# A layer of selected experts on one core: sums, splits and conditions at other places

## The chip, the cores and the metric

The kernel runs on one NeuronCore of a Trainium2 chip. The metric is the device time of one execution in microseconds. A core has TensorE (PE, with its weight loads shown apart as PEld), VectorE (DVE), ScalarE (ACT), GpSimd (POOL) and SyncE (SP). Each takes its instructions in its own order and waits on semaphores; SP only issues DMAs here.

## What is computed

`x` is 128 rows of 64 tokens of 256 numbers (float32). There are five routed experts, one chosen per row by `itok`, and two shared experts that every token passes. Each is a dense layer of 256 to 1024, a relu, and one of 1024 to 256.

```python
def _L0_cond_ref(x, type_label, wi, wo, swi, swo, g1, g2):
    s0 = _dense(x, swi[0], swo[0])          # relu(x @ wi) @ wo
    s1 = _dense(x, swi[1], swo[1])
    h = jax.nn.relu(jnp.einsum('bsd,bdf->bsf', x, wi[type_label]))
    eo = jnp.einsum('bsf,bfd->bsd', h, wo[type_label])
    gate_in = jnp.concatenate([eo[:, 0], s0[:, 0], s1[:, 0]], axis=-1)
    w = jax.nn.softmax(jax.nn.relu(gate_in @ g1) @ g2, axis=-1)[:, :, None, None]
    return eo * w[:, 0] + s0 * w[:, 1] + s1 * w[:, 2]

x = x + _L0_cond_ref(x, itok, ...)
# then one step of diffusion: y is x seen as 128 grids of 64 x 256, reflected at the borders
x = x + zX * lap_x(y) + zY * lap_y(y) + zR * y * (1.0 - y)
```

## The kernel before, in words

**Numbers in two parts.** A product in float32 precision is made of three PE matmuls: every operand is split in a high part (fp32r) and a low part, and high x high, high x low and low x high are added up. A split is one ACT copy (high part) and one subtraction on DVE or POOL (low part). What the relu gives is split likewise: in `hidden`, ACT's relu writes the high part and a DVE `scalar_tensor_tensor` the low part.

**Items and units.** Work on 512 tokens by one expert is an item. Its first layer isn't done as 8 products of blocks but by a scheme with 7 products (`A11` to `S4` of weights, `B11` to `T4` of tokens), which needs sums of weight blocks (`wsum`, `sum_wi`) and of token blocks (`xt`, `sum_x`) in advance. An item has four units (`unit`, q = 0 to 3). Each makes 7 products of 3 matmuls 128x512 into three PSUM tiles pa, pb and pd:

- pa = A11 B11; ACT copies it into pb
- pb += S2 T2; ACT copies pb to u2 in SBUF (records call it u); pa += A12 B21 gives the unit's first hidden tile
- pb += S3 T3 (after the u2 copy, since it writes the same tile), pd = S1 T1; ACT copies pb to u3; DVE adds c22 = pd + u3
- pb += A22 T4 gives a hidden tile, c22 is another; pd += S4 B22 (after c22, which reads pd), and pd + u2 is the fourth

The relu and low part of the fourth are put in the list `late` and issued after the first ACT copy of the next unit. Between the products stand the second layer's matmuls of the unit before (`gaps`, matmuls acc<-wo,h). They are 512 columns wide for the high part of h, 256 for the low part, which comes last. At an item's end the rows of the second half of tokens (`h_0b` to `h_7b`) follow, row after row into new PSUM tiles. Six PSUM tiles rotate for pa, pd and the accumulators, two for pb.

**Hooks.** Everything else is issued at fixed places in the program: `at(k, work)` puts work at hook k mod 4 of unit k // 4 of the item. `run(hooks[j])` stands in `unit`; hooks 16 and 17 are after the fourth unit. The order on every engine is then the program's order (`Ordered.on`, `keep`).

**Sequence.** Items 0 and 1 are the two shared experts on the first 512 tokens (to about 86 us), then five items of routed experts, numbered from EI = 100 (about 86 to 294 us, 41.57 us each), then a stream of nine smaller groups of rows (`stream(0, NRUN)`, about 294 to 443 us). In it each group takes 8 steps f: `up` (first layer, plain), `down` (second layer) two steps later, and `ahead` for loads and splits of the next group. Groups have 8 rows or 4; group 3 (HALF) is half as wide as the narrow ones (2 rows, 128 columns). In the stream ACT's, DVE's and POOL's instructions aren't held in program order (`in_order(False)`): a scheduler places them, PE's and the DMAs keep theirs. Groups 9 to 11 are needed only when the rows fall badly among the experts; a condition on a value read from the table (`total[0]`) guards them, and they don't run with these inputs. Then the shared experts' other token tiles are items 2 to 15 (41.34 us each), in which the outputs of the routed experts are gathered by POOL, summed with the gates, diffused (`diffuse_a`: ACT and POOL; `diffuse_b`: three DVE steps per half) and stored.

**Names in the records.** `wi` and `wsr`: split and raw weights; `x` and `xr`: split and raw tokens; `xt`: token sums; `gw`, `gwr`, `gh`, `gacc`: weights, raw weights, hidden and accumulators of the groups; `lq`, `la`, `lb`: the diffusion's tiles; h_0 to h_7 with a or b: hidden tiles of an item, a for the first half of the tokens. A matmul recorded as acc<-wo,h_0b reads such a tile. Nearly all records carry line 93 (`mm`) or line 108 (`keep`), so that tiles tell them apart; the condition is line 1124.

Of the kernel before, what the change touches and what calls it, by code (L numbers as in the profile page):

```python
# [21 lines left out]
NB = 4  # L22
# [27 lines left out]
def cond_resid_kernel(ctx: ExitStack, tc: tile.TileContext, xg, xs, xn, itok, z, we, ws, g1, g2, out):  # L50
# [580 lines left out]
    def product(dst, w, i, x, start, stop):  # L631
        for j, (wp, xp) in enumerate(((0, 0), (0, 1), (1, 0))):
            mm(dst, w[:, wp, i, :], x[:, xp, :], start and j == 0, stop and j == 2)

    def hidden(store, key, src):
        h = slot4(f"h{key[0]}_{key[1]}{'ab'[store is hb]}")
        act.activation(h[:, 0, :], src, AF.Relu)
        vec.scalar_tensor_tensor(h[:, 1, :], src, 0.0, h[:, 0, :].bitcast(F32), ALU.max, ALU.subtract)
        store[key] = h
# [9 lines left out]
    def unit(n, q, gaps, hooks):  # L649
        p = tokens(n)  # L650
        w = wip.pop(n * NQ + q)
        f = 2 * q
        pa = psum(f"pa{n}_{q}")
        pb = seeded(f"pb{n}_{q}")
        product(pa, w, A11, xop[p, B11], True, False)
        act.activation(pb, pa, AF.Copy)
        finish_late()
        run(gaps[0])
        run(hooks[0])
        product(pb, w, S2, xop[p, T2], False, False)  # L660
        product(pa, w, A12, xop[p, B21], False, True)
        u2 = slot2(f"u2_{n}_{q}")
        act.activation(u2, pb, AF.Copy)
        hidden(ha, (n, f), pa)
        run(gaps[1])
        run(hooks[1])
        product(pb, w, S3, xop[p, T3], False, False)
        pd = psum(f"pd{n}_{q}")
        product(pd, w, S1, xop[p, T1], True, False)
        u3 = slot2(f"u3_{n}_{q}")  # L670
        act.activation(u3, pb, AF.Copy)
        c22 = slot2(f"c22_{n}_{q}")
        vec.tensor_tensor(c22, pd, u3, ALU.add)
        run(gaps[2])
        run(hooks[2])
        product(pb, w, A22, xop[p, T4], False, True)
        product(pd, w, S4, xop[p, B22], False, True)
        hidden(hb, (n, f + 1), c22)
        hidden(ha, (n, f + 1), pb)
        vec.tensor_tensor(pd, pd, u2, ALU.add)  # L680
        late.append(lambda: hidden(hb, (n, f), pd))
        run(hooks[3])

# [270 lines left out]
    def ahead(g, f):  # L954

        if g >= NRUN:
            return
        if f == 0:
            if g == NRUN - 3:
                slots = nc.values_load(  # L960
                    tab[0:1, NSLOT + NU : NSLOT + NU + 1], min_val=0, max_val=NSLOT,
                    skip_runtime_bounds_check_because="the table's entries are bounded on the chip",
                )
                total.append(slots)
            if g + 1 < NRUN:
                if g <= NBIG and g != HALF:
                    load_group_w(g + 1)
                if g != HALF:
                    load_group_x(g + 1)
            if g < 2:  # L970
                reload(g)
            for u in range(3 * g, min(3 * g + 3, 2 * NQ)):
                load_wo(u)
            if g == NRUN - 2:
                load_x(1)
            if g == NRUN - 1:
                load_wi(2, 0)
                load_wi(2, 1)
                load_row()
        if f == 5 and g < 2:  # L980
            again(g)
        if g + 1 == HALF and f == 4:
            load_group_x(g + 2)
        if f == 6 and (g + 1 == HALF or NBIG <= g < NRUN - 2):
            load_group_w(g + 2)
        if g == 0 and f + FIRST < NF:
            split_group_w(0, f + FIRST)
        if g == HALF + 1 and f + 6 < NF:
            split_group_w(g, f + 6)
        if g + 1 < NRUN:  # L990
            if f == (0 if g == HALF else 4):
                split_group_x(g + 1)
            if g != HALF or f < 6:
                split_group_w(g + 1, f)
        elif f < 7:
            if f < 4:
                sum_x(1, T1 + f, gps)
            split_x(1, (B11, B21, T2, T3, T1, T4, B22)[f], vec)
# [19 lines left out]
    def at(k, *work):  # L1018

        return {divmod(k, 4): list(work)}  # L1020
# [64 lines left out]
    def next_fours(n, sums, splits):  # L1085
# [12 lines left out]
        at(3, lambda: load_fours(EI)),  # L1098
        at(8, lambda: dma(zt, z)),
        at(11, clear_spare, lambda: dma(g1t, g1), lambda: dma(g2t, g2)),  # L1100
        next_fours(EI, (10, 12, 14, 15), (15, 16, 16, 16, 16, 17, 17)),
    )
    left = item(1, left, bg)

# [16 lines left out]
    in_order(False)  # L1121
    stream(0, NRUN)

    with tc.If(total[0] > UH * NB):  # L1124
        for g in range(NRUN, NG):
            load_group(g)
            split_group_x(g)
            for f in range(NF):
                split_group_w(g, f)
            stream(g, g + 1)  # L1130
# [13 lines left out]
    def next_x(p):  # L1144
        if p == NP:
            return {}
        if p == 2:
            sums, splits, eng, slow = (8, 9, 10, 11), (12, 15, 14, 16, 16, 17, 16), gps, (B11, B21, B22)
        else:
            sums, splits, eng, slow = (10, 12, 14, 15), (15, 16, 16, 16, 16, 17, 17), vec, (B22,)  # L1150
        return join(
            at(4, lambda: load_x(p)),
            *(at(k, lambda i=i: sum_x(p, i, eng)) for i, k in zip((T1, T2, T3, T4), sums)),
            *(
                at(k, lambda i=i: split_x(p, i, gps if i in slow else vec))
                for i, k in zip((B11, T2, B21, T3, T1, T4, B22), splits)
            ),
        )

    def diffusion(t, k, with_halo=True, second=3, steps=(0, 1, 2)):  # L1160
        parts = [at(k, lambda: halo(t))] if with_halo else []
# [23 lines left out]
    for p in range(1, NP):  # L1185
        ta, tb = 2 * p, 2 * p + 1
        for e in range(2):
            n = 2 * p + e
            parts = [ahead_w(n)]
            if n == 2:  # L1190
                load_gate()
                parts.append(at(0, gate_shared))
                parts.append(at(1, gate_hidden_s))
                parts.append(at(4, lambda: load_y(0)))
                parts.append(at(5, step_factors))
                parts.append(at(4, gate_expert))
                parts.append(at(6, gate_hidden_e, lambda: load_y(2)))
                parts.append(at(7, lambda: load_sh(0)))
                parts.append(at(8, lambda: load_eo(0)))
                parts.append(at(9, lambda: load_y(3)))  # L1200
                parts.append(at(10, gate_weights))
                parts.append(sums(0, 11))
                parts.append(at(12, lambda: load_eo(2)))
                parts.append(at(13, lambda: load_y(1)))
                parts.append(at(16, lambda: load_sh(1)))
                parts.append(starts(ta, 17, 0))
            elif n == 3:
                parts.append(at(0, lambda: load_eo(3), lambda: load_eo(1)))
                parts.append(sums(1, 1))
                parts.append(starts(tb, 5))  # L1210
                parts.append(diffusion(0, 7, True, 4))
                parts.append(at(12, lambda: halo(1)))
                parts.append(next_x(2))
            elif n == 4:
                parts.append(at(2, lambda: load_y(4)))
                parts.append(diffusion(1, 0, False))
                parts.append(at(6, lambda: load_eo(4)))
                parts.append(diffusion(2, 6))
                parts.append(at(9, lambda: load_y(5)))
                parts.append(at(11, lambda: load_eo(5)))  # L1220
                parts.append(starts(ta, 14))
                parts.append(starts(tb, 16, 0))
            elif e == 0:
                parts.append(at(0, lambda t=ta: load_y(t), lambda t=ta: load_eo(t)))
                parts.append(at(4, lambda t=tb: load_y(t), lambda t=tb: load_eo(t)))
                parts.append(diffusion(ta - 2, 2))
                parts.append(starts(ta, 10))
                parts.append(starts(tb, 13))
            else:
                parts.append(diffusion(ta - 1, 2))  # L1230
                parts.append(next_x(p + 1))
            if n == 2 * NP - 1:
                parts.append(at(4, lambda: load_last(n)))
                parts.append(at(8, lambda: split_last_w(n)))
                parts.append(at(9, lambda: split_last_x(n)))
                parts.append(at(10, diagonals))
                parts.append(at(12, lambda: halo(ta)))
            left = item(n, left, join(*parts))
# [38 lines left out]
```

## Time and profile before

| | us |
|---|---|
| median of 3 executions | 1040.71 (1039.96 to 1044.65) |
| the profiled execution | 1041.6 |
| its span, from the first to the last record | 1039.9 |
| granted PE clock | 1.00 |
| idle time of DVE ahead of c (c22), mostly until ACT's u | 43.7 |
| idle time of ACT ahead of u, mostly until PE's pb | 111.0 |

The profile is of one execution. A row of the timeline is "start, duration, engine, line, operation, output<-inputs, shape, count", with the idle time before it and what ended it in brackets; one row may stand for several instructions. A row of the waits is "engine, tile, line <- engine, tile, line: us in all, times, longest". A matmul's record lasts longer than the distance to the next one, since matmuls are pipelined; the distance between two starts is what it costs.

Three stretches matter for the change. The table of busy times by stretch has them in this order: the half-width group, the condition, the second shared item (length, then busy time and instructions of each engine):

```profile
core 0: us, PE busy (x) PEld busy (x) DVE busy (x) ACT busy (x) POOL busy (x), PEclk, DMA share, GB/s
363.30:376.10 12.80, 11.89 (x88) 10.92 (x87) 10.97 (x26) 8.88 (x24) 0.00 (x0) 1.00 0.78 255
441.30:445.20 3.90, 1.88 (x12) 1.42 (x10) 0.76 (x2) 0.38 (x1) 0.00 (x0) 1.00 0.04 8
70.50:84.00 13.50, 12.67 (x63) 10.16 (x62) 12.91 (x28) 8.44 (x20) 0.00 (x0) 1.00 0.99 348
```

### The profile page before, as it was taken

To read this page: it belongs to the slowest core of one execution; us is meant where nothing else is said; L and a number is where in the kernel's file an instruction comes from. 1 tells how busy PE (TensorE), PEld (TensorE's weight loads), DVE (VectorE), ACT (ScalarE), POOL (GpSimd) and SP (SyncE) were. 2 spreads that over 40 slices of the span, in tenths; PEclk is the share of its full clock that TensorE was granted. 3 is DMA by queue.
4 is the path that set the end of the run, shared out by engine and by line. 5 is a ranking of instruction groups with operands and counts; after the bars stand their busy time and mean duration, and the time that the engine had idled before them with its cause. 6 is when DMAs were issued, how large, how long until landed. Compare 5 with 4: busy or idle time off the path is not lost.

```text
span 1039.9 us, 15667 instructions
## 1 busy us (share of the span) xinstructions
PE 1030.5 (99%) x5423; PEld 882.1 (85%) x5423; DVE 810.6 (78%) x1502; ACT 571.5 (55%) x1080; POOL 154.3 (15%) x165
## 2 busy tenths in 40 slices
PE   9999999999999999999999999999999999999998
PEld 7878888888888889978888888888888888888888
DVE  7997977988768575747889778678688688688776
ACT  6476666776656565643654545446355364355362
POOL 3000000000013100211432220212212102022020
PEclk9999999999999999999999999999999999999999
DMA  6477233331458765556435435334344163253321
GB/s 217 173 269 249 77 104 94 105 122 52 132 170 307 271 207 172 181 182 219 158 127 177 137 110 200 122 122 167 112 168 154 65 227 122 81 191 138 117 77 46
DMA packets 67123, 159.15 MB, mean 153 GB/s; under 512 B 7680, under 2 KB 34688, under 8 KB 67040
## 3 DMA queue, kind: packets, MB, share of 16 engines
q1 hardware_dynamic: 64512, 149.46, 41.8%
q0 software_dynamic: 2384, 8.52, 2.5%
q8 instruction: 44, 0.72, 0.3%
q14 instruction: 39, 0.32, 0.1%
q10 hardware_dynamic: 144, 0.13, 0.0%
HBM read 126.75 MB, written 31.33 MB: 152 GB/s over the span
## 4 chain that ended last, share of the span: by engine, by line
PE 57%; DVE 0%; ACT 0%; issue 0%; DVEq 0%
PE acc L93 30%; PE pb L93 11%; PE pd L93 7%; PE pa L93 7%; PE pu L93 1%; PE lin_b L93 0%; PE pgs L93 0%; PE gacc L93 0%; PE lin_c L93 0%; PE pge L93 0%; DVE lq L108 0%; DVE c L108 0%; ACT pb L108 0%; DVE end_qb L108 0%; PE pl L93 0%
## 5 line engine op out<-in xcount | busy, mean ns | idle before, releaser
L93 PE MATMUL pb<-x,wi 128*128 128x512 f32 x729 | 208.0, 393 | 0.6 <-ACT u L108 0.3
L108 ACT ACTIVATE u<-pb 128x512 f32<-128x512 f32 x162 | 96.9, 598 | 111.0 <-PE pb L93 107.9
L93 PEld LDWEIGHTS pb<-x,wi 128*128 128x128 f32 x729 | 130.4, 189 | 26.0 <-ACT u L108 3.5
L93 PE MATMUL pd<-x,wi 128*128 128x512 f32 x486 | 137.9, 392 | 0.1
L93 PE MATMUL pa<-x,wi 128*128 128x512 f32 x486 | 136.9, 390 | 0.0
L108 DVE SCALAR_TENSOR_TENSOR yb<-acc,wgt,yb 128x256 f32<-128x256 f32 x216 | 99.3, 482 | 18.1 <-PE acc L93 14.3
L108 ACT ACTIVATE pb<-pa 128x512 f32<-128x512 f32 x81 | 47.2, 582 | 115.5 <-PE pa L93 114.6
L93 PEld LDWEIGHTS pd<-x,wi 128*128 128x128 f32 x486 | 90.9, 188 | 21.9 <-DVE c L108 1.9
L93 PEld LDWEIGHTS pa<-x,wi 128*128 128x128 f32 x486 | 89.9, 188 | 17.8
L108 DVE TENSOR_TENSOR c<-pd,u 128x512 f32<-128x512 f32 x81 | 55.9, 690 | 43.7 <-ACT u L108 32.6
L93 PE MATMUL up<-gxh,gw 128*128 128x512 f32 (+2 forms) x288 | 73.4, 329 | 0.0
L108 POOL TENSOR_TENSOR la<-yb 128x508 f32<-128x508 f32 (+1 forms) x28 | 32.2, 1150 | 260.5 <-ACT yb L108 259.0
L93 PE MATMUL gacc<-gw,gh 128*128 128x512 f32 (+1 forms) x272 | 60.7, 363 | 2.9 <-PEq L1124 2.0
L93 PEld LDWEIGHTS gacc<-gw,gh 128*128 128x128 f32 x272 | 47.4, 188 | 11.6 <-issue 2.3
L93 PE MATMUL acc<-wo,h_0b 128*128 128x256 f32 (+1 forms) x172 | 56.5, 332 | 0.6 <-DVE h_6b L108 0.6
L108 DVE TENSOR_TENSOR gw<-gwr,gw 128x512 fp32r<-128x512 f32 x72 | 53.1, 780 | 5.0 <-ACT gw L108 4.9
L93 PE MATMUL acc<-wo,h_6b 128*128 128x256 f32 (+1 forms) x172 | 56.7, 334 | 0.0
L93 PE MATMUL acc<-wo,h_1b 128*128 128x256 f32 (+1 forms) x172 | 56.7, 333 | 0.0
L93 PE MATMUL acc<-wo,h_7b 128*128 128x256 f32 (+1 forms) x172 | 56.7, 333 | 0.0
L93 PE MATMUL acc<-wo,h_2b 128*128 128x256 f32 (+1 forms) x172 | 56.6, 333 | 0.0
L93 PE MATMUL acc<-wo,h_5b 128*128 128x256 f32 (+1 forms) x172 | 56.5, 332 | 0.0
L93 PE MATMUL acc<-wo,h_4b 128*128 128x256 f32 (+1 forms) x172 | 56.5, 332 | 0.0
(254 smaller groups left out, 2458.3 us busy)
## 6 DMA issues: line engine op xcount, KB each, us to landing
wi<-wi_d SPq DMA_DIRECT2D x55, 896.0 KB, 4.6
gwr<-we_in SPq DMA_DIRECT2D x32, 512.0 KB, 5.0
wsr<-we_in SPq DMA_DIRECT2D x20, 512.0 KB, 5.2
xr<-xs_in SPq DMA_DIRECT2D x32, 256.0 KB, 5.2
yb<-xn_in SPq DMA_DIRECT2D x16, 512.0 KB, 5.8
y_out<-lq SPq DMA_DIRECT2D x30, 256.0 KB, 2.2
wi_d<-wi SPq DMA_DIRECT2D x8, 896.0 KB, 4.5
xr<-xg_in SPq DMA_DIRECT2D x80, 64.0 KB, 2.0
```

The costliest lines, as they stand in the source:

```text
L93: nc.tensor.matmul(out_ap, lhsT=lhsT, rhs=rhs, start=start, stop=stop, skip_group_check=True)
L108: ins = call(*args, **kwargs)
```

## The change

1. In `unit`, pd += u2 stands ahead of the two `hidden` calls whose low parts DVE makes, so that on DVE the sum comes first. The `hidden` of pd itself stays in `late`.
2. In `ahead`, while group 3 (the half-width one) runs, weights of group 4 are split for f = 0 to 3 and no longer for 0 to 5; during group 4 the parts f + 4 are split and not only f + 6.
3. In item 1, three of the four token sums for the first routed item go one hook earlier (12, 14, 15 become 11, 12, 14), and the split of B11 goes from hook 15 to 16.
4. Each of the three seldom-run groups has a condition of its own, with the same test.
5. In item 4 the diffusion of tiles 1 and 2 is placed by the new function `diffusion_at`: the first half of tile 1 keeps its hooks, its second half's steps go from 5, 6, 7 to 6, 6, 7; the steps of tile 2 go from 8, 9, 10 and 11, 12, 13 to 8, 10, 10 and 11, 12, 14. `halo(2)` is issued behind the load at hook 6, not with the diffusion.

PE's order of matmuls stays as it was. On SP two stores of a routed item's output are issued two token loads later, and branches are added on every engine.

```diff
@@ unit
         product(pd, w, S4, xop[p, B22], False, True)
+        vec.tensor_tensor(pd, pd, u2, ALU.add)
         hidden(hb, (n, f + 1), c22)
         hidden(ha, (n, f + 1), pb)
-        vec.tensor_tensor(pd, pd, u2, ALU.add)
         late.append(lambda: hidden(hb, (n, f), pd))
@@ ahead
-        if g == HALF + 1 and f + 6 < NF:
-            split_group_w(g, f + 6)
+        if g == HALF + 1 and f + 4 < NF:
+            split_group_w(g, f + 4)
         if g + 1 < NRUN:
             if f == (0 if g == HALF else 4):
                 split_group_x(g + 1)
-            if g != HALF or f < 6:
+            if g != HALF or f < 4:
                 split_group_w(g + 1, f)
@@ item 1
-        next_fours(EI, (10, 12, 14, 15), (15, 16, 16, 16, 16, 17, 17)),
+        next_fours(EI, (10, 11, 12, 14), (16, 16, 16, 16, 16, 17, 17)),
@@
-    with tc.If(total[0] > UH * NB):
-        for g in range(NRUN, NG):
+    for g in range(NRUN, NG):
+        with tc.If(total[0] > UH * NB):
             load_group(g)
             split_group_x(g)
             for f in range(NF):
@@
+    def diffusion_at(t, starts, steps):
+
+        parts = []
+        for half in range(2):
+            parts.append(at(starts[half], lambda half=half: diffuse_a(t, half)))
+            for step in range(3):
+                parts.append(at(steps[half][step], lambda half=half, step=step: diffuse_b(t, half, step)))
+        return join(*parts)
@@ item 4
-                parts.append(diffusion(1, 0, False))
+                parts.append(diffusion_at(1, (0, 3), ((2, 3, 4), (6, 6, 7))))
                 parts.append(at(6, lambda: load_eo(4)))
-                parts.append(diffusion(2, 6))
+                parts.append(at(6, lambda: halo(2)))
+                parts.append(diffusion_at(2, (6, 9), ((8, 10, 10), (11, 12, 14))))
```

## The prediction

> **What bounds the kernel now.** I read the page's busy line and chain first. The chain names the engine that sets the end.
>
> ```profile
> PE 1030.5 (99%) x5423; PEld 882.1 (85%) x5423; DVE 810.6 (78%) x1502; ACT 571.5 (55%) x1080; POOL 154.3 (15%) x165
> ...
> PE 57%; DVE 0%; ACT 0%; issue 0%; DVEq 0%
> ```
>
> TensorE is busy 99% of a span of 1039.9 us and nothing else stands in the chain. No matmul is added or removed, so only PE's gaps can change. A busy share hides them, because a record lasts longer than the step to its successor: in the timeline of PE, steady matmuls start every 0.227 us with 512 columns (0.39 recorded) and every 0.120 us with 256. I took each start-to-start distance above these: 12.95 us in all. From the sixth token item on (after 560 us) there are only about 0.07 us per item of 41 us, so the change has nothing to win there, apart from 0.8 us at the tail, which it doesn't touch. Next came the lists of waits, of PE and of its weight loads, where a matmul's wait is often booked:
>
> ```profile
> PE gacc L93 <- PEq L1124: 2.0, 1, 2.0
> ...
> PE gacc L93 <- DVE gh L108: 0.9, 1, 0.9
> PE acc L93 <- DVE h_6b L108: 0.6, 1, 0.6
> ```
>
> ```profile
> PEld pb L93 <- ACT u L108: 3.5, 9, 0.7
> ...
> PEld pd L93 <- DVE c L108: 1.9, 5, 0.5
> ```
>
> Each is a place: the condition; the half-width group; the second shared item; the S3 product waiting for ACT's copy u (u2), which frees its PSUM tile; S4 waiting for c22. After each gap the second matmul comes another 0.11 late. The touched gaps, in us lost: 59.05 us (0.39), 74.72 (0.53), 102.08 (0.225), 144.0, 185.6, 227.1 (0.15 each), 268.7 (0.16), 517.1 (0.12), all S3; 83.87 (0.85, h_6b); 375.79 (1.16, gh); 445.13 (2.27, condition); 553.95 (0.38, c22). Together 6.5 us: the most that can be won.
>
> [...] 44 instruction packets of 16,384 B, one about every 24 us, and one at 442.22 us inside PE's branch, whose record runs from 441.225 for 3.73 us. [...] ACT's and DVE's records say 50 and 72 ns, but 0.45 and 0.59 us pass until their next instruction; I use those.
>
> **The change, part by part** (plus is slower).
>
> 1. *u2 ahead of the low parts.* Removed: two DVE operations between S4 and the sum. ACT's relu of pd, and the next unit's u2 copy queued behind it, come up to 1.2 us earlier.
>
> ```profile
> ACT h_6b L108 <- DVE pd L108: 23.6, 20, 1.7
> ```
>
> So the S3 gaps go: 0.84 in the routed items (102 to 269 us), 0.12 at 517, 0.92 in the shared items (counted in part 2). Added: the sum needs PE's last S4 matmul, the low parts did not. DVE waits in order, so everything behind waits too. Last unit of the second routed item:
>
> ```profile
> 161.72 0.69 DVE L108 TENSOR_TENSOR xt<-xr 128x512 f32<-128x512 f32 x1
> 162.33 0.69 DVE L108 SCALAR_TENSOR_TENSOR h_7b<-c,h_7b 128x512 fp32r<-128x512 f32 x1
> 162.93 0.69 DVE L108 SCALAR_TENSOR_TENSOR h_7a<-pb,h_7a 128x512 fp32r<-128x512 f32 x1
> 163.53 0.69 DVE L108 TENSOR_TENSOR pd<-pd,u 128x512 f32<-128x512 f32 x1
> ...
> 166.27 0.68 DVE L108 SCALAR_TENSOR_TENSOR h_6b<-pd,h_6b 128x512 fp32r<-128x512 f32 x1
> ```
>
> ```profile
> 161.91 0.85 PE L93 MATMUL pd<-x,wi 128*128 128x512 f32 x3
> ...
> 167.19 0.40 PE L93 MATMUL acc<-wo,h_0b 128*128 128x512 f32 x1
> ```
>
> DVE is free at 162.33; S4 starts at 161.91, and where c22 waits for such a product of three matmuls, DVE begins 0.97 after its start (PE at 451.87, DVE at 452.84 in the timeline): the sum starts at 162.88, and DVE runs 0.55 late. It has no idle until h_6b, which moves from 166.95 to 167.50. PE's matmul at 167.19 opens a new accumulator in the PSUM tile that pd leaves, so it waits for this very h_6b. New gap: 167.50 + 0.06 for the signal (h_6b ends at 83.81 and its matmul starts at 83.87) − 167.19 = 0.37, plus 0.11: 0.48, in the first four routed items (the fifth and the token items have no weight and token sums in between, and keep over 0.5 us of slack). 4 × 0.48 = +1.9. Routed items: −0.84 + 1.9 = **+1.07**. In other units c22 is 0.69 us ahead of S4 against a shift of 0.36 to 0.55, covered, and every unit starts anew from its own S4. Ends: −0.84 (margin half a microsecond larger than I read) and +2.5.
>
> 2. *Second shared item.* Three token sums and one split move a hook (a quarter of a unit), so DVE's work is spread differently; its stretch from 70.5 to 84 us is busy for 12.91 of 13.50. The first sum still waits for its DMA until 70.54. From there the new order is continuous: sum T1, pd's sum 71.15, two low parts, weight sums, T2, h_4b, wi, T3, h_6a, wi, c22 from 77.42 to 78.11, 0.6 later than now. PE would reach S4 at 77.85 − 0.92 = 76.93 with the S3 gaps gone, and starts it at 78.16 instead: the 0.92 is given back, and 0.31 more. But h_6b, now one sum shorter, ends before PE asks, so the 0.74 at 83.87 goes, and one restart stays. Row 1 starts at 83.54 rather than 83.87, its restart of 0.11 gone: **−0.44**. Ends −1.1 (c22 in time) and +0.3 (h_6b late as well).
>
> 3. *Half-width group.* Two splits of the next group's weights, 0.60 us each on DVE, move behind. From 363.3 to 376.1 us DVE is the limit (busy for 10.97 of 12.80, the rest mostly one wait of 1.83 for ACT's ge at 368.61): a split 0.6 each, a low part 0.2. Here the scheduler orders the instructions by itself, and the new order has 8 splits and 4 low parts ahead of the awaited gh, where there were 9: 375.03 rather than 375.65. The 1.16 becomes about 0.56: **−0.6**. Ends: −1.16 and 0. The two splits fall in the next group, where PE has no gap over 0.1 us.
>
> 4. *Conditions.* None of the groups runs here.
>
> ```profile
> 441.31 1.80 PE L93 MATMUL gacc<-gw,gh 128*128 128x512 f32 x9
> 445.13 1.06 PE L93 MATMUL gacc<-gw,gh 128*128 128x512 f32 x4 [2.02 <-PEq L1124]
> ```
>
> [...] two more near jumps, partly beside it, cost up to 0.59 each. **+0.4**. Ends: −1.4 (all near: 3 × 0.59 instead of the branch) and +2.4 (the third fetch begins only when it is reached).
>
> 5. *Fifth token item's diffusion.* The same DVE steps at other hooks. Those of 1.4 to 1.6 us stand beside POOL's work; the usual is 0.7. c22 at 553.22 was 1.0 late. Some move behind it, others stay ahead: between −0.38 (gone) and +0.5 (again a long one ahead); **+0.1**. Two stores of SP move two loads later, which nothing near awaits: 0.
>
> 6. 517 us: **−0.12**. All else nothing, under cover of PE.
>
> Sum: 1.07 − 0.44 − 0.6 + 0.4 + 0.1 − 0.12 = +0.4 us. The profiled execution took 1041.6 us (1.7 beyond its span): it would take 1042.0. It lies 0.9 above the median shown (1040.71), so for a median I say 1041.1.
>
> **Rivals.** (a) *All gaps go and no new one comes.* For: PE has the slack list above, ACT waits 23.6 us for pd. Against: DVE's free time of 162.33. Parts 1 to 3 and 5 at their good ends: −0.84 − 1.1 − 1.16 − 0.38 − 0.12 = −3.6, with the conditions at −1.4: −5.0. Time 1035.7 to 1037.1. (b) *Slower: every branch costs PE a full fetch.* At the condition; price 3.7 us each, 11.1 instead of 3.7: +7.4, time 1048. [...] For: the one jump recorded did fetch. [...] (c) *The new row-1 wait is larger*, the signal from PE coming 0.3 later in five items: +1.5, time 1042.6. (d) *The half-width group isn't relieved*, the scheduler putting its splits ahead again: +0.6, time 1041.7.
>
> **How the numbers follow.** Forecast with (c) and (d), all within a few us: 0.70; (a) 0.17, of which 0.10 beyond the bound, since its best end lies 0.2 us short of it and runs of one kernel spread over 4.7 us; (b) 0.13. A difference of 0.5% (5.2 us) is what a measurement of this kernel can tell from none. Faster 0.10, same 0.76, slower 0.14 ((b), and 0.01 of spread). The range reaches to the best of (a), 1035.5, and, for the bad ends of 1 (+1.4), 4 (+2.0) and the run-to-run spread, to 1045.5.
>
> **What would show it.** Right: no wait of S3 for u, the row-1 wait for h_6b (0.3 to 0.5 us) in four routed items, PE's wait in the half-width group near 0.4, three branches with one fetch and matmuls again at 445.5 less what was won before. Wrong: no wait for h_6b at the routed items; two or three fetches in a row at the conditions; a steady item that differs from its 41.34 us.

## The result, and the profile after

The changed kernel takes 1043.99 us (median of 18 runs, 1043.11 to 1045.94), the kernel before 1040.90 us (18 runs beside them). The ratio is 1.0029 with a 95% interval from 1.0022 to 1.0036: 2.3 to 3.7 us slower. The profiled span grew from 1039.9 to 1042.8 us.

The busy line of the changed kernel's page:

```profile
PE 1031.4 (99%) x5423; PEld 881.3 (85%) x5423; DVE 806.9 (77%) x1502; ACT 569.2 (55%) x1080; POOL 153.4 (15%) x165
```

The instructions are the same in number and PE is as full as before. As predicted, only its gaps can tell. What its matmuls and weight loads wait for in the changed kernel:

```profile
PE gacc L93 <- PEq L1125: 2.0, 1, 2.0
...
PE pd L93 <- DVE h_2b L108: 1.2, 1, 1.2
PE pu L93 <- DVE h_5a L108: 0.6, 1, 0.6
...
PE gacc L93 <- DVE gh L108: 0.2, 1, 0.2
```

```profile
PEld pd L93 <- DVE c L108: 2.3, 6, 0.8
...
PEld acc L93 <- DVE h_6b L108: 2.2, 4, 0.6
...
PEld pb L93 <- ACT u L108: 1.0, 2, 0.6
```

Against the lists of before: the weight loads' nine waits for u (3.5 us) have become two (1.0), the wait for gh went from 0.9 to 0.2, and that at the condition stayed. New are four waits for h_6b where there was one, one for h_2b and one for h_5a; a smaller one, for h_4b (0.4 us), is in the second shared item. The order of the matmuls is the same in both kernels, so the distance between the same two matmuls' starts can be set side by side. All stretches that differ by more than 0.1 us, that of the condition, and the sum (us between the starts of the same matmuls, the stretch named by its time in the kernel before):

| stretch | before | after | difference | predicted |
|---|---|---|---|---|
| start to 22 | 22.22 | 22.42 | +0.20 | 0 |
| 22 to 60, first and second shared item | 37.86 | 37.47 | −0.39 | −0.39 |
| 60 to 85, second shared item | 25.05 | 25.45 | +0.40 | −0.05 |
| 85 to 275, routed items | 190.00 | 190.85 | +0.85 | +1.07 |
| 360 to 380, half-width group | 19.92 | 19.52 | −0.40 | −0.6 |
| 380 to 446, condition | 65.90 | 65.84 | −0.06 | +0.4 |
| 480 to 520, third and fourth token item | 40.04 | 39.76 | −0.28 | −0.12 |
| 549 to 556, diffusion of the fifth token item | 7.03 | 8.13 | +1.10 | +0.1 |
| 556 to 1000, eleven token items | 443.94 | 444.14 | +0.20 | 0 |
| 1000 to 1012, ahead of the last unit | 12.07 | 13.16 | +1.09 | 0 |
| all | | | +2.71 | +0.4 |

The predicted column splits the −0.44 of the prediction's second part over the two rows that it covers. Two rows hold 2.19 of the 2.71 us, and the prediction had next to nothing in either. Each column is one execution, so a difference counts only where the stretch repeats. Over the profiles of all twelve kernels of this document it does in most rows: where a part isn't changed, 85 to 275 us takes 189.91 to 190.07, 360 to 380 takes 19.92 to 19.96, 549 to 556 takes 7.03 to 7.04 and 1000 to 1012 takes 12.07 each time. It doesn't in the first row (21.8 to 24.0 us over the twelve), nor in that of 60 to 85 us, to which I come back below.

**The end.** DVE's timeline of the changed kernel, where the last unit of seven products hands over to the plain tile, and PE's:

```profile
1010.11 0.69 DVE L108 TENSOR_TENSOR c<-pd,u 128x512 f32<-128x512 f32 x1
1011.86 0.70 DVE L108 TENSOR_TENSOR pd<-pd,u 128x512 f32<-128x512 f32 x1 [1.06 <-PE pd L93]
1012.46 0.68 DVE L108 SCALAR_TENSOR_TENSOR h_5b<-c,h_5b 128x512 fp32r<-128x512 f32 x1
1013.06 0.69 DVE L108 SCALAR_TENSOR_TENSOR h_5a<-pb,h_5a 128x512 fp32r<-128x512 f32 x1
```

```profile
1011.66 1.53 PE L93 MATMUL pu<-x,wi_plain_last 128*128 128x512 f32 x6
1013.80 1.66 PE L93 MATMUL pu<-x,wi_plain_last 128*128 128x512 f32 x6 [0.61 <-DVE h_5a L108]
```

The same place in the kernel before:

```profile
1008.13 0.68 DVE L108 TENSOR_TENSOR c<-pd,u 128x512 f32<-128x512 f32 x1
1009.51 0.69 DVE L108 SCALAR_TENSOR_TENSOR h_5b<-c,h_5b 128x512 fp32r<-128x512 f32 x1 [0.70 <-ACT h_5b L108]
1010.12 0.68 DVE L108 SCALAR_TENSOR_TENSOR h_5a<-pb,h_5a 128x512 fp32r<-128x512 f32 x1
1010.72 0.69 DVE L108 TENSOR_TENSOR pd<-pd,u 128x512 f32<-128x512 f32 x1
```

```profile
1009.87 2.88 PE L93 MATMUL pu<-x,wi_plain_last 128*128 128x512 f32 x12
```

In the changed kernel DVE stands idle for 1.06 us in front of the sum, until S4 ends. It stood idle here before as well, 0.70 us for ACT's h_5b. From the start of c to that of h_5a it was 1.99 us and is now 2.95: 0.36 more of idle time and 0.60 for the sum itself. The plain tile's second half takes the pb tile that h_5a reads, and its first matmul comes 0.06 us after h_5a ends (1013.06 + 0.69). Before, h_5a was done 0.4 us before PE asked (1010.80 against 1011.23, the seventh of the twelve matmuls at 0.227 us each). What follows the sum decides: in the items from 582 to 1004 us it waits 0.38 to 0.98 us in each unit, and the stretch from 556 to 1000 us is only 0.20 longer in all, with no new gap over 0.02 us.

**The diffusion.** DVE and PE of the changed kernel near 550 us:

```profile
545.06 0.69 DVE L108 TENSOR_TENSOR c<-pd,u 128x512 f32<-128x512 f32 x1 [0.73 <-ACT u L108]
545.67 1.50 DVE L108 TENSOR_TENSOR lq<-lq,yb 128x512 f32<-128x512 f32 x1
547.28 1.78 DVE L108 SCALAR_TENSOR_TENSOR lq<-la,zt,lq 128x512 f32<-128x512 f32 x1
548.98 0.69 DVE L108 TENSOR_TENSOR pd<-pd,u 128x512 f32<-128x512 f32 x1
...
551.02 1.37 DVE L108 SCALAR_TENSOR_TENSOR lq<-lb,zt,lq 128x512 f32<-128x512 f32 x1
552.32 0.68 DVE L108 SCALAR_TENSOR_TENSOR h_2b<-pd,h_2b 128x512 fp32r<-128x512 f32 x1
```

```profile
551.00 0.84 PE L93 MATMUL pb<-x,wi 128*128 128x512 f32 x3
553.05 0.96 PE L93 MATMUL pd<-x,wi 128*128 128x512 f32 x3 [1.21 <-DVE h_2b L108]
```

And DVE of the kernel before:

```profile
544.74 0.69 DVE L108 TENSOR_TENSOR c<-pd,u 128x512 f32<-128x512 f32 x1
545.35 1.50 DVE L108 SCALAR_TENSOR_TENSOR lq<-la,zt,lq 128x512 f32<-128x512 f32 x1
...
548.57 1.57 DVE L108 SCALAR_TENSOR_TENSOR lq<-lb,zt,lq 128x512 f32<-128x512 f32 x1
550.06 0.68 DVE L108 SCALAR_TENSOR_TENSOR h_2b<-pd,h_2b 128x512 fp32r<-128x512 f32 x1
```

Between c and h_2b there are three steps on lq, 4.65 us together, where before there were two (1.50 and 1.57). h_2b is the last reader of a pd tile, which PE wants back 0.7 us after 551.00.

### The profile page after: what moved, and what is told of

Same layout as the page of the kernel before. It is cut to its first block, busy times and chain, and to the rows that moved or that the text cites. A ratio compares the mean times of both kernels' runs of the same rounds, so it can differ in the third digit from the quotient of the medians.

```text
span 1042.8 us, 15737 instructions
## 1 busy us (share of the span) xinstructions
PE 1031.4 (99%) x5423; PEld 881.3 (85%) x5423; DVE 806.9 (77%) x1502; ACT 569.2 (55%) x1080; POOL 153.4 (15%) x165
## 5 line engine op out<-in xcount | busy, mean ns | idle before, releaser
L108 DVE TENSOR_TENSOR pd<-pd,u 128x512 f32<-128x512 f32 x81 | 56.6, 699 | 44.9 <-PE pd L93 44.8
L108 POOL TENSOR_TENSOR la<-yb 128x508 f32<-128x508 f32 (+1 forms) x28 | 29.5, 1054 | 266.1 <-ACT yb L108 263.5
```

Of the source, the lines that this page charges most:

```text
L108: ins = call(*args, **kwargs)
```

## The experiments

Each kernel ran beside the kernel before on the same chip. Times are ratios to it with a 95% interval; the stretches are from the profiles, as in the table above.

### The parts by themselves

The sum alone (`e1_u2_only`), everything but the sum (`e2_all_but_u2`), the diffusion alone (`e3_diffusion_only`), the half-width group alone (`e4_half_only`). The edits are those parts of the diff shown above; the sum's is

```diff
         product(pd, w, S4, xop[p, B22], False, True)
+        vec.tensor_tensor(pd, pd, u2, ALU.add)
         hidden(hb, (n, f + 1), c22)
         hidden(ha, (n, f + 1), pb)
-        vec.tensor_tensor(pd, pd, u2, ALU.add)
```

> The kernel before with the sum pd + u2 moved ahead of the two low parts, and nothing else. Theory (the sum waits for S4, and what DVE has queued behind it comes late to a PSUM tile): the row-1 wait for h_6b of about 0.40 us in each of the first four routed items (+1.6), their S3 gaps gone (-0.7), the last item's wait for h_5a ahead of its plain tile (+1.0), the S3 and c22 gaps of 504 and 517 us gone (-0.4), the shared items -0.4 to 0: about +1.1 us in all. Rival (the losses of the changed kernel come from the diffusion's new places, the sum only removes gaps): -1.5 us, with no wait for h_6b or h_5a.

> The changed kernel with the sum put back behind the two low parts; the four other parts stay. Theory: half-width group -0.6, conditions 0, diffusion about +1.1 to +1.5, sums of the second shared item between -0.4 and +0.3: about +0.7 us against before, no wait for h_6b in the routed items and none for h_5a at the end. Rival (the sum's place is the cause of the stall near 551 us too): -0.8 us, and no stall near 551 us.

> The kernel before with the diffusion of the fifth token item at the new places, and nothing else. Theory: between c22 near 544.7 us and h_2b there are three diffusion steps on DVE rather than two, 1.4 to 1.8 us each beside POOL; h_2b has 0.6 us of slack before PE's pd product needs its PSUM tile, so a stall of about 1.2 us comes at 551 us, and the 0.38 at 554 goes: +0.8 to +1.1 us. Rival (that stall needs the sum ahead of the low parts): -0.4 to 0 us.

> The kernel before with two fewer splits during the half-width group, and nothing else. Theory: the wait for gh near 375.8 us goes from 1.16 to about 0.5 us, -0.6 us. Rival (the scheduler puts the splits ahead again, or the wait moves to the next group): 0.

| kernel | ratio | 22–60 | 60–85 | 85–275 | 360–380 | 480–520 | 549–556 | 1000–1012 |
|---|---|---|---|---|---|---|---|---|
| before | | 37.86 | 25.05 | 190.00 | 19.92 | 40.04 | 7.03 | 12.07 |
| sum alone | 1.0015 (1.0007 to 1.0022) | 37.46 | 25.19 | 190.79 | 19.96 | 39.72 | 7.08 | 13.16 |
| all but the sum | 1.0008 (0.9999 to 1.0017) | 37.82 | 24.32 | 189.92 | 19.44 | 40.03 | 8.65 | 12.07 |
| diffusion alone | 1.0011 (1.0003 to 1.0020) | 37.86 | 24.43 | 190.07 | 19.94 | 40.04 | 8.66 | 12.07 |
| half-width group alone | 0.9995 (0.9989 to 1.0002) | 37.84 | 25.01 | 190.07 | 19.47 | 40.05 | 7.03 | 12.07 |

The sum alone makes both new waits, in the routed items (+0.79) and at the end (+1.09), and alone has the gains at 22 to 60 and 480 to 520. The rival that it only removes gaps falls. Without the sum, the stall near 550 us is there all the same and larger: +1.62 rather than +1.10. So it belongs to the diffusion's places, and the sum ahead of the low parts even softens it. The timelines of PE and ACT in the diffusion-only kernel show by which way it comes then:

```profile
549.26 0.39 PE L93 MATMUL acc<-wo,h_3a 128*128 128x512 f32 x1
551.37 0.96 PE L93 MATMUL pb<-x,wi 128*128 128x512 f32 x3 [1.72 <-ACT u L108]
```

```profile
550.23 0.60 ACT L108 ACTIVATE h_2b<-pd 128x512 fp32r<-128x512 f32 x1 [3.14 <-DVE pd L108]
550.72 0.59 ACT L108 ACTIVATE u<-pb 128x512 f32<-128x512 f32 x1
```

The sum comes behind the long diffusion steps, ACT's relu of pd waits for it, u waits behind that relu in ACT's queue, and S3 waits for u. With the sum ahead, u is in time and the next wait, h_2b's, is the one that shows. The half-width group wins 0.45 in its stretch; its ratio reaches from 1.1 us faster to 0.2 slower, so the time by itself doesn't tell it from nothing.

### The sum in the last item alone

```diff
+        first = n == 2 * NP - 1
+        if first:
+            vec.tensor_tensor(pd, pd, u2, ALU.add)
         hidden(hb, (n, f + 1), c22)
         hidden(ha, (n, f + 1), pb)
-        vec.tensor_tensor(pd, pd, u2, ALU.add)
+        if not first:
+            vec.tensor_tensor(pd, pd, u2, ALU.add)
```

> The kernel before with the sum ahead of the two low parts in the last item alone. Theory: in its third unit the sum waits about 1 us for S4, so h_5a's low part, which reads pb, ends about 2 us later, after PE wants that PSUM tile for the plain tile: a wait of about 0.8 us there and 0.1 to 0.3 of restarts and c22, +1.0 us, and no difference of any size elsewhere. Rival (the wait at the end of the changed kernel was the execution's, not the order's): 0.

Ratio 1.0011 (1.0002 to 1.0020). The stretch from 1000 to 1012 takes 13.16 us, as in the changed kernel to the hundredth, and the stretches from 520 to 1000 are those of before. One line moved in this item's three units costs 1.09 us. Its PE waits have the same row as the changed kernel's:

```profile
PE pu L93 <- DVE h_5a L108: 0.6, 1, 0.6
```

### What makes h_6b late in the routed items

On top of the changed kernel, the weight sums of a routed item's last unit behind h_6b:

```diff
-                parts.append(at(4 * q + 3, lambda u=behind[1]: sum_wi(u, vec)))
+                k = 16 if q == NQ - 1 and n >= EI else 4 * q + 3
+                parts.append(at(k, lambda u=behind[1]: sum_wi(u, vec)))
```

> The changed kernel with the four weight sums of the last unit of each routed item (1.1 us on DVE, between pd's sum and h_6b) moved behind h_6b, to hook 16. Theory (h_6b is late by what DVE has queued behind the waiting sum): the four row-1 waits of 0.40 us go, -1.6 us against the changed kernel, about +1.3 us against before. Rival (PE waits there for something else of the new order, such as ACT's relu): the waits stay, 0 against the changed kernel.

First the changed kernel's DVE in the last unit of the second routed item, then the same place with the weight sums moved:

```profile
163.00 0.70 DVE L108 TENSOR_TENSOR pd<-pd,u 128x512 f32<-128x512 f32 x1 [0.39 <-PE pd L93]
...
164.81 0.28 DVE L108 TENSOR_TENSOR wsum<-wsr 128x128 f32<-128x128 f32 x1
...
166.95 0.68 DVE L108 SCALAR_TENSOR_TENSOR h_6b<-pd,h_6b 128x512 fp32r<-128x512 f32 x1
```

```profile
163.51 0.70 DVE L108 TENSOR_TENSOR pd<-pd,u 128x512 f32<-128x512 f32 x1 [0.38 <-PE pd L93]
...
166.52 0.68 DVE L108 SCALAR_TENSOR_TENSOR h_6b<-pd,h_6b 128x512 fp32r<-128x512 f32 x1
...
168.67 0.28 DVE L108 TENSOR_TENSOR wsum<-wsr 128x128 f32<-128x128 f32 x1
```

The wait in front of the sum is the same (0.39 and 0.38 us), but h_6b starts 3.01 us after it and not 3.95, and the four waits of PE are gone. The routed items take 189.18 us: 1.67 less than in the changed kernel (four times 0.40 was expected) and 0.82 less than before. Here the earlier sum wins what it was worth. The ratio against before is 1.0008 (0.9999 to 1.0017), since the losses at 550 us and at the end are still in it.

### One diffusion step put back

On top of the diffusion-only kernel:

```diff
-                parts.append(diffusion_at(1, (0, 3), ((2, 3, 4), (6, 6, 7))))
+                parts.append(diffusion_at(1, (0, 3), ((2, 3, 4), (5, 6, 7))))
```

> The diffusion-only kernel with one step put back: the first step of tile 1's second half at hook 5, ahead of c22, as before, rather than at hook 6; tile 2 stays at its new hooks. Theory (one diffusion step too many between c22 and h_2b): no stall near 551 us, and the gap of 0.38 at 554 stays gone, -0.4 us against before, -2.0 against the diffusion-only kernel. Rival (the stall comes from tile 2's places or from POOL's work beside it): it stays, +1.6 us against before.

DVE of this kernel at the same place:

```profile
543.23 0.68 DVE L108 TENSOR_TENSOR lq<-lq,yb 128x512 f32<-128x512 f32 x1
543.94 0.69 DVE L108 TENSOR_TENSOR c<-pd,u 128x512 f32<-128x512 f32 x1
544.55 1.49 DVE L108 SCALAR_TENSOR_TENSOR lq<-la,zt,lq 128x512 f32<-128x512 f32 x1
...
547.77 1.57 DVE L108 SCALAR_TENSOR_TENSOR lq<-lb,zt,lq 128x512 f32<-128x512 f32 x1
549.26 0.68 DVE L108 SCALAR_TENSOR_TENSOR h_2b<-pd,h_2b 128x512 fp32r<-128x512 f32 x1
```

549 to 556 takes 6.65 us: 2.01 less than with the step at hook 6, 0.38 less than before, both as expected. The step ahead of c takes 0.68 us; behind c it took 1.50 in the changed kernel, beside POOL's work from 545.58 us on. Where POOL stood still, three steps of the same form took 0.68, 0.74 and 0.74 us (539.00 to 543.51 us in the kernel before). Beside POOL in the changed kernel, the step of 1.50 us ended 0.55 us after the POOL operation that had begun before it (547.17 against 546.62), while the sum and h_3a, which read a PSUM tile, kept their 0.69 and 0.68 us. So the long steps go with POOL's work; that it is their cause is not shown, since no run here took that work away. Tile 2's new places are a gain of 0.38 (c22 isn't late at 554 us). With tile 2 at its new places, all of the loss is the one step that went from hook 5 to 6. The ratio, 0.9997 (0.9988 to 1.0006), is too wide to show 0.4 us.

### The conditions, and the token sums

> The kernel before with a condition for each of the three groups, and nothing else. Theory: PE's third branch waits for the same fetch as the one branch before, its matmuls resume after a gap of about 2.2 us: 0 to +0.2 us. Rival (the branches cost more than the changed kernel's one execution showed): +1 us or more.

> The kernel before with the token sums and the split of the second shared item at the new hooks, and nothing else. Theory: with the sum of pd behind the low parts, the new hooks lengthen the second shared item's second half by no wait, and h_6b comes in time: PE needs 24.3 us from 60 to 85 us, where kernels with the old hooks needed 24.4 to 25.1 in the profiles so far: -0.4 us. Rival (the hooks are the reason of the 25.5 us in the changed kernel): 25 us or more, +0.3 us.

With three conditions and nothing else the ratio is 0.9996 (0.9990 to 1.0003), and PE's wait at the condition 1.9 us, as before (2.0). No cost shows. The trace of the changed kernel has the three branches on PE: 0.36, 0.22 and 1.18 us long, where the one of before was 3.73, with about 2 us of idle PE either way; an instruction packet is at 442.95 us, between the first and the third. From start to start, PE's matmuls are 2.0 to 2.5 us apart here in the eight kernels with one condition and 2.3 to 2.4 in the four with three.

With the new hooks alone the ratio is 0.9999 (0.9989 to 1.0010), and 60 to 85 us takes 24.72. That misses the 24.3 expected and doesn't bear out the rival's 25. The six kernels with the old hooks and the old place of the sum in this item took 24.38 to 25.05 (mean 24.69), those with the new hooks and the sum in its old place 24.32 and 24.72, and the three with the sum ahead throughout 25.19, 25.45 and 24.93 (mean 25.19). By these means the sum would cost half a microsecond here and the hooks nothing. But the length goes with something else: when the first token sum, which waits for its loads, can start. Counted from the stretch's first matmul, it starts after 10.76 to 11.24 us in the three with the sum ahead and after 9.94 to 11.00 in the six; and the one of the six with 11.00, the half-width group alone, took 25.01 with neither part in it. The changed kernel has the latest start of all twelve (11.24; 10.45 before). Nor is the 0.39 us that the earlier sum wins at 59 us seen any more at 85: from 22 to 85 us the four kernels that have that gain took 62.35 to 62.92 (mean 62.6), the eight others 62.15 to 62.91 (mean 62.5). PE then reaches the loads earlier, and they land no earlier: the first token sum, which waits for them, starts at 70.54 us before and at 71.13 in the changed kernel. So these profiles show no gain in this stretch and no loss that belongs to the order of the sum or to the hooks; what the two parts do there stays open.

### The parts that are of use, together

The sum is ahead only where it won (routed items, the fourth token item, the first unit of the second shared item); the weight sums go behind h_6b; tile 1's diffusion has its old hooks. The fewer splits, the new token sums and tile 2's new hooks stay, and there is one condition.

```diff
+        first = EI <= n or n == 3 or (n == 1 and q == 0)
+        if first:
+            vec.tensor_tensor(pd, pd, u2, ALU.add)
```

> The kernel before with what the runs so far showed to be of use: the sum ahead of the low parts in the routed items, in the fourth token item and in the first unit of the second shared item only; weight sums of a routed item's last unit behind h_6b; fewer splits in the half-width group; the new token sums; tile 2's diffusion at the new hooks and tile 1's at the old ones; one condition. Theory: each part keeps what it showed alone: -0.4 (22 to 60 us), -0.4 (60 to 85), -0.8 (routed items), -0.5 (half-width group), -0.3 (480 to 520), -0.4 (554 us): -2.8 us against before, and no new wait. Rival (the parts aren't independent, one early gain is given back at a later wait): -1.5 us or less.

1039.01 us against 1041.45 on the same chip, ratio 0.9977 (0.9970 to 0.9984): 1.7 to 3.1 us faster than before, and so faster than both. By stretches: −0.41 (22 to 60), +0.02 (60 to 85), −0.81 (routed items), −0.46 (half-width group), −0.27 (480 to 520), −0.38 (549 to 556): −2.3 us. Five of the six expected gains came, the token sums' again didn't. Nor did "no new wait" come quite: the longest wait of a weight load for u, in the second shared item, is 1.1 us, and in the kernel before none was over 0.7.

## Why the prediction was right, and where it failed

*Right in what it said of the whole:* no change clear of half a per cent (it gave that 0.76), a time within its range, and PE's gaps as the only place to look. It said +0.4 us where +3.1 was measured, and its words on what can be told were too wide: with 18 runs of each, the interval of 0.22 to 0.36% is clear of nothing. That the time fell inside the range is in part luck. The upper end was made of bad ends of parts 1 and 4 and of the spread of runs; those bad ends didn't come, and two losses that it hadn't seen took their room.

*Part 1, routed items: right.* A wait for h_6b of 0.37 + 0.11 us was predicted in four items; 0.30 + 0.11 came in just those four (the sum began 0.89 us after S4's start, 163.00 against 162.11, not 0.97). +1.07 said, +0.85 measured; moving the weight sums out of DVE's queue removed it.

*Part 1, "every unit starts anew from its own S4", and the tail "which it doesn't touch": wrong, 1.09 us.* This is the step that failed. The mechanism was the one already worked out for the routed items, but it was followed only to h_6b. The question who takes the tile that the delayed low part reads was not put at the other place where an item doesn't go on with an equal unit: the last item's third unit. There pb's tile is the one wanted, h_5a was 0.4 us ahead of PE, and it comes 0.96 us later after c than before. "c22 is 0.69 us ahead of S4", which was to cover the rest, doesn't hold there either: c ended at 1010.80 and S4 started at 1010.86. Putting the sum ahead in that item alone showed the whole loss.

*Part 5, diffusion: wrong in size, +0.1 said (at most +0.5), +1.10 measured.* The estimate watched c22 of the next unit, the wait that the profile of before showed there, and that one went, as the end of −0.38 had it. It didn't count what the moved step delays on its way: the two readers of pd between, the sum and h_2b, which in the kernel before were 0.6 us ahead of PE. One step put back removed 2.01 us.

*Part 2, second shared item: wrong by 0.45 in this execution.* The chain of DVE operations came in the predicted order; it began with the DMA at 71.13 and not at 70.54, and S1 waited for h_4b (0.42 us), a pd tile again. The gap at h_6b went as said. Of the two S3 gaps there the one of 0.39 went, but of the 0.53 at 74.72 us 0.44 stayed: in ACT's queue u stands behind a split of weights, which waited for a DMA (0.20 us). So the sign "no wait of S3 for u" came only in part.

*Part 3, half-width group: right,* −0.6 said, −0.40 here and −0.45 alone. *Part 4, conditions: +0.4 said, 0 measured.* The +0.4 was the author's estimate, from the 0.59 us that pass on DVE from a branch to its next instruction. In the trace two of PE's branches took 0.36 and 0.22 us, and only the third was longer, 1.18 us. An instruction packet started about 1 us behind the first branch (442.95 against 441.89), as one did behind the single branch (442.22 against 441.23), and the price was the old one: the third branch ends 2.6 us after the start of that packet, the single one 2.7. The two short branches added nothing: the first was done at 442.25, before PE had worked off its matmuls (443.78), the second at 444.18, before the packet had ended (444.21). That the long branch waits for the packet is a reading of these times; no run shows it apart. The part's lower end of −1.4 doesn't follow from its own figures either, 3 × 0.59 instead of 3.73 being −1.96. *Part 6: −0.12 said, −0.28 measured;* c22 at 504 us came in time as well.

*The rivals.* (b), a full fetch at each branch, falls. (a), no new waits, falls too. (c) is the nearest, that the sum's wait costs more than counted; but it costs more in other places than it named. (d), a half-width group that isn't relieved, falls by the −0.40 and −0.45.

## What to carry to other kernels

When an operation that waits for a later event is moved ahead of others on an in-order engine, follow every operation behind it to the buffer that it releases, and do this at each place where the sequence breaks off or changes, not only in the steady state and where a gap shows today. A wait absent from the profile of before may be 0.4 us away. And see what else stands between the waiting operation and the one that is needed: here, moving four small sums behind h_6b turned the same change in the routed items from a loss (+0.85) into a gain (−0.82).

A gain ahead of a place that waits for a DMA may not last: that of 0.39 us at 59 us was gone by 85.

## What the runs showed of the hardware

After PE's gap of about 2 us at the condition, six of the twelve profiles, of kernels with one condition or three alike, have PE's clock halved for 3.4 us, beginning 0.1 to 1.4 us after the gap (with the half-width group alone, the granted clock is 0.62 from 444 to 446 us, 0.52 from 446 to 448 and 1.00 from 448 to 450). The table by stretch of the sum-alone kernel, with length, busy times and granted clock:

```profile
446.00:449.00 3.00, 2.50 (x10) 2.19 (x11) 0.74 (x2) 0.68 (x2) 0.00 (x0) 0.76 0.02 5
449.00:450.50 1.50, 1.50 (x6) 1.09 (x5) 0.23 (x2) 0.58 (x1) 0.00 (x0) 0.50 0.52 174
```

The matmuls from 446 to 449 us of before then take 4.0 to 4.3 us rather than 3.14. The kernels before and after show it in neither of their profiles, and it lies in none of the stretches that the tables compare. It is in the times, though, and as large as each effect studied here. The six profiled executions with it have a mean clock of 0.998 over the whole, the six others 0.999 or 1.000; and of the 136 executions of the kernel before that stand beside the experiments, 51 have 0.998 or less, and their medians are 0.95 to 1.65 us above those of the others. So a part of each ratio's width is how many such executions a kernel happened to have. With those at 0.999 and 1.000 alone, the half-width group by itself is 0.5 us faster in the median (13 runs against 35), as its stretch says. What decides whether the clock halves is not shown. The length of the gap alone doesn't: PE's idle time was 1.8 to 2.1 us where the clock halved and 1.6 to 2.0 where it didn't. The next longest, 1.7 us near 551 us in two of the kernels, was followed by no halving, which two executions don't settle.
